# Two attentions on one core: norm scales placed behind the second multiplication, opening output products split, 32-row loads placed ahead of a store

## The chip, the cores and the metric

The kernel runs on one core of a Trainium2 chip. A core has TensorE (PE in the profile), VectorE (DVE), ScalarE (ACT), GpSimd (POOL) and SyncE (SP, which here only issues DMAs). Each has its own queue of instructions, worked through in order, and they meet only through semaphores. The metric is the time of one execution on the device, in microseconds (us); less is better.

## The reference

The input x holds 8 sequences of 512 tokens with 512 channels in fp32. The context holds 8 sequences of 120 tokens, which both attentions read.

```python
x = x + jnp.tanh(g_xattn[0]) * _L0_xattn_ref(_layernorm(x), ctx_1024, ctx_1024, ...)
x = x + jnp.tanh(g_ffn[0])   * _L0_ffn_ref(_layernorm(x), ...)
x = x + jnp.tanh(g_xattn[1]) * _L1_xattn_ref(_layernorm(x), ctx_1024, ctx_1024, mask, ...)
x = x + jnp.tanh(g_ffn[1])   * _L1_ffn_ref(_layernorm(x), ...)

# attention (the second has biases and a key mask besides)
q, k, v = split_heads(Q @ W_q.T), split_heads(K @ W_k.T), split_heads(V @ W_v.T)   # 16 heads of 32
probs = softmax(einsum('bhqd,bhkd->bhqk', q, k) / sqrt(32))
out = einsum('bhqk,bhkd->bhqd', probs, v) @ W_o.T

# first feed-forward: per group of 32 tokens and per expert column, the token with the largest logit
perm = (logits == max(logits over the 32 tokens of the group))
inner = relu(einsum(perm-selected tokens, W1) + b1);  result = perm-scattered (inner @ W2 + b2)

# second feed-forward: a channel mix with a one-token shift
out = sigmoid(xr @ W_r.T) * (square(relu(xk @ W_k.T)) @ W_v.T)
```

## The kernel before

The 4096 tokens are 32 tiles of 128 rows (NT = 32), four to a sequence (TB = 4). x stays on the chip, tokens on the partitions. The two attentions run one after the other and share one class; attention 1 takes about 73 to 430 us of the profiled run and attention 2 about 711 to 1010. Between them lies the routed feed-forward, behind them the channel mix.

**A slot.** Each attention is a loop over tiles; one pass is called a slot, and slot k starts with the scores of tile k on PE. The slots 4 to 27 are `steady(k)`, and the order in which it emits work is the order in each engine's queue: nothing reorders it later. In a slot PE does the scores of tile k (`s`, preceded in attention 2 by a mask product), the output product of tile k-3 (`output`, `ops`: 4 chunks of 128 channels), the query products of a later sequence, transposes of x and of the normalized x (`rxps`, `xnps`), the routing logits (`rlps`), and the product of probabilities and values of tile k-2 (`attend`, `aps`). The number k%4 (f in the code) decides which query products a slot has, so slots differ in length with it.

**The softmax.** The scores lie in two halves, u = 0 and 1. DVE takes the maxima (`largest`, L710), ACT does eight exponentials a half with their sums (L721), DVE takes the reciprocal of the sums (L727), and POOL multiplies the probabilities with it (`divide`, L731). Half 1 goes first: `divide(1)`, then `divide(0)`, the second multiplication of probabilities.

**Turning the probabilities.** For tiles 4 to 25 (`CROSSED`) the probabilities are not transposed on PE. The 120 keys of a head are stored as 4 blocks of 30, each padded to 32. DVE transposes blocks of 32x32 (`turn_blocks`, L793), SP stores the halves to a buffer in device memory (`plane<-pr`, L796), and four loads bring it back with keys on the partitions (`fetch_blocks`, L806, `prT<-plane`), each of 30 rows that lie 4 partitions apart. Half 1 of tile k is turned and stored in slot k, half 0 in slot k+1; then the loads follow. There is one buffer `prT`, so the loads wait until `attend` of the tile before is done; two wide `pr` buffers alternate, so the exponentials of tile k+2 wait until the stores of tile k have landed.

**Queries.** The query products use a scheme with seven products p1 to p7 for a block of 2x2 (Strassen's, in Winograd's form). Its sums fall to POOL (L110, L203, L204) and DVE (L183, L212), and L177 on ACT copies p1. Each product's PSUM tile comes from the same small rotation of banks (`tag="mm"`) as `ops`, `rxps`, `xnps` and `aps`, so each of those waits until the engine that read the bank's last tenant is done.

**Norm scales.** When a tile's output has been added to x, DVE takes its mean and variance (`layernorm_sums`, L52 and L53), and POOL turns them into a scale and an offset with three small instructions (`layernorm_scales`, L61, L62, L64: `ve`, `rstd`, `nmr`). In attention 1 this is `RoutedFfn.in_slot`: at the stage "final" x is put aside to device memory (L1046) and the statistics and scales are made; at the stage "late" ACT applies them in place (`route_scale`, L1052), as the last thing that the slot puts into ACT's queue before the next slot's exponentials. In attention 2 it is `ChannelMix.in_slot`: the statistics come at "final", the scales at "late", four tiles at a time in every fourth slot.

**The opening.** Slot 4 is the first steady one. Before the change it does the whole output of tile 2 in its middle and `attend(3)` at its end; slot 5 does no output in the middle and two chunks of tile 3's output at its end; slot 6 does the other two chunks in its middle; from slot 7 on the pattern is regular.

Of the kernel before, what the change touches and what calls it, by code (L numbers as in the profile page):

```python
# [19 lines left out]
LK = 120  # L20
NH, HD = 16, 32
NT = B * S // P
TB = S // P
NC = D // P
# [8 lines left out]
KB, KF = 4, 30  # L33
# [15 lines left out]
def layernorm_sums(cm, pool, t):  # L49

    st = pool.tile([P, 6], FP, name="bnst")
    cm.nc.vector.bn_stats(st, cm.x[:, t, :])  # L52
    cm.nc.vector.bn_aggr(cm.mv[:, t, :], st)  # L53


def layernorm_scales(cm, pool, t, n):

    nc, ts = cm.nc, slice(t, t + n)
    mean, rstd, nmr = cm.mv[:, ts, 0], cm.rstd[:, ts, 0], cm.nmr[:, ts, 0]
    ve = pool.tile([P, TB], FP, name="ve")[:, :n]  # L60
    nc.gpsimd.tensor_scalar(ve, cm.mv[:, ts, 1], EPS, None, ALU.add)  # L61
    nc.gpsimd.tensor_tensor(rstd, ve, cm.mhalf.to_broadcast([P, n]), ALU.pow)  # L62
    if n == 1:
        nc.gpsimd.tensor_scalar(nmr, mean, rstd, -1.0, ALU.mult, ALU.mult)  # L64
    else:
        nc.gpsimd.tensor_tensor(nmr, mean, rstd, ALU.mult)
        nc.gpsimd.tensor_scalar(nmr, nmr, -1.0, None, ALU.mult)
# [153 lines left out]
class CrossAttention:  # L221
# [566 lines left out]

    def turn_blocks(self, t, u):

        nc = self.nc
        pr = self.probs[t][:, u * 1024 : (u + 1) * 1024]
        nc.vector.transpose(pr, pr)  # L793
        if u == 1:
            self.planes[t] = self.dram.tile([KB, P, 2, 256], FP, name="plane")
        nc.sync.dma_start(  # L796
            out=self.planes[t][:, :, u, :].rearrange("k p e -> p k e"),
            in_=pr.rearrange("p (k e) -> p k e", k=KB),
        )

    def fetch_blocks(self, t):

        prT = self.late.tile([P, 4, 512], FP, name="prT", bufs=1)
        plane = self.planes.pop(t).rearrange("k (q f) u e -> k f q (u e)", q=4)
        for k in range(KB):
            self.nc.sync.dma_start(out=prT[k:LK:KB], in_=plane[k, :KF])  # L806
        self.probs[t] = prT

    def transpose_probs(self, t):
# [118 lines left out]
    def steady(self, k):  # L928

        b, f = divmod(k + TB, TB)  # L930
        crossed = k in CROSSED
        if k == TB:
            self.transpose_probs_late(k - 1)
        largest, exponentials, divide = self.softmax(k, self.score_products(k))
        for u in (1, 0):
            largest(u)
        if k - 1 in CROSSED:
            self.turn_blocks(k - 1, 0)
        done = {TB: TB - 2, TB + 1: None}.get(k, k - 3)
        if done is not None:  # L940
            self.output(done, range(2 if done == TB - 1 else 0, NC))
        exponentials(1)
        divide(1)
        if done is not None:
            self.after(done, "final")
        exponentials(0, range(4))
        if f == 0:
            self.begin_queries(b)
        self.q7.postponed = True
        self.q7.next()  # L950
        exponentials(0, range(4, 8))
        if crossed:
            self.turn_blocks(k, 1)
        self.q7.settle(1)
        divide(0)
        if f != TB - 1:
            self.q7.next()
        if f == 0:
            self.sum_tokens(2)
        self.q7.settle()  # L960
        self.after(k, "route")
        if k + 8 < NT:
            self.transpose_x(k + 8)
        if k == TB:
            self.attend(k - 1)
        elif k == TB + 1:
            self.output(TB - 1, range(2))
        else:
            self.attend(k - 2)
        if k - 1 in CROSSED:  # L970
            self.fetch_blocks(k - 1)
        if k + 9 < NT:
            self.normalize(k + 9)
        if done is not None:
            self.after(done, "late")

    def tail(self):

        for k in range(NT - TB, NT + 2):
            self.transpose_probs_late(k - 2)  # L980
            rest = self.scores(k) if k < NT else []
            self.output(k - 3, range(NC))
            self.after(k - 3, "final")
            self.after(k, "head")
            for part in rest:
                part()
            self.after(k, "route")
            self.attend(k - 2)
            self.after(k - 3, "late")
            self.after(k, "end")  # L990
        self.output(NT - 1, range(NC))
        self.after(NT - 1, "final")
        self.after(NT - 1, "late")
        self.after(NT + 2, "end")


class RoutedFfn:
# [42 lines left out]

    def route_stats(self, t):
        layernorm_sums(self.cm, self.route, t)
        layernorm_scales(self.cm, self.route, t, 1)

    def put_aside(self, t):
# [53 lines left out]
    def in_slot(self, s, attention, stage):  # L1099

        if stage == "final":
            self.put_aside(s)
            self.route_stats(s)
        if stage == "late":
            self.route_scale(s)
        if stage == 2 and 0 <= s - 1:
            self.route_stats(s - 1)
            self.route_norm(s - 1)
        if stage not in (1, "route"):
            return  # L1110
        pool = attention.p_mm
        if s == -1:
            self.start()
        if stage == "route":
            s -= 1
        if 0 <= s - 4:
            self.route_logits(s - 4, pool.tile([P, D], FP, name="rlps", tag="mm"))
        if 0 <= s - 3:
            self.route_x(s - 3, pool.tile([P, D], FP, name="rxps", tag="mm"))
        b, i = divmod(s - 8, TB)  # L1120
        if i == 0 and 0 <= b < B - 2:
            self.route_back(b, pool.tile([P, D], FP, name="pps", tag="mm"))
# [256 lines left out]
class ChannelMix:  # L1379
# [56 lines left out]
    def in_slot(self, s, attention, stage):  # L1436

        nc = self.nc
        self.at = attention
        if stage == 2 and s >= 1:  # L1440
            attention.stats(s - 1)
        if stage == "final" and s < NT - 2 * TB:
            attention.stats(s, False)
        if stage == "late" and s < NT - 2 * TB:
            attention.scales(s)
        if s == -1:
            self.start()
        if stage == "head" and s == NT:
            self.sum_value_weights()
            self.k7.next()  # L1450
        if stage == "end" and s == NT + 1:
            for c in range(NC):
                self.mix_chunk(0, 0, c)
            self.k7.next()
        if stage == "end" and s == NT + 2:
            for step in self.sum_steps(0, 0):
                step()
            self.k7.next(2)
            self.sum_gate_weights()
            for t in range(TB, 2 * TB):  # L1460
                self.normalize(t)
        if stage != "route":
            return
        if s == TB + 1:
            nc.vector.tensor_scalar(self.om, self.mu, -1.0, 1.0, ALU.mult, ALU.add)
        i = s - (NT - 9)
        if 0 <= i - 1 < TB:
            self.transpose(i - 1)
        if 0 <= i < TB:
            xn = self.at.norm.tile([P, D], FP, name="xn")  # L1470
            self.normalize(i, xn)
        if s == NT - 4:
            wv = self.at.pool.tile([P, NC, D], FP, name="wv", tag="wq")
            self.wv = self.load(wv, self.ins[2])
            self.weight_sums = self.sum_key_weights()
        if 0 <= s - (NT - 5) < NC:
            self.mix_chunk(0, 1, s - (NT - 5))
        if s in (NT - 4, NT - 3):
            for _ in range(2):
                self.weight_sums.pop(0)()  # L1480
        if s == NT - 2:
            self.key_sums = self.sum_steps(0, 1, nc.gpsimd)
        if s in (NT - 2, NT - 1):
            for _ in range(2):
                self.key_sums.pop(0)()
        if s == NT - 1:
            self.k7 = self.keys(0)
            self.k7.next()
        if s in (NT, NT + 1):
            self.k7.next()  # L1490
# [336 lines left out]
```

## Time and profile before

| | us |
|---|---|
| median of 3 runs | 1346.75 (1345.57 to 1349.14) |
| the profiled execution | 1344.31 |
| its span | 1342.5 |
| PE busy | 1291.0 (96%) |
| DVE busy | 1002.2 (75%) |
| ACT busy | 807.1 (60%) |
| POOL busy | 704.6 (52%) |
| mean granted TensorE clock | 0.999 |

The profile comes from one execution, whose own time is the 1344.31 us; the span is the stretch between its first and last recorded instruction. An engine's busy time says how long it worked, not whether its work was on the path that sets the end: for that one reads who waited for whom. In lines of the timeline the columns are start (us), duration (us), engine, source line, operation, output<-inputs, shapes and count; in square brackets stands how long the engine had been idle before it, and what released it. Small idle times are partly lost in the modelled ends of PE's instructions.

Lengths of the slots 8 to 24 in this execution, start of scores to start of scores:

| k%4 | attention 1 | attention 2 |
|---|---|---|
| 0 | 10.96 (10.52 in slot 24) | 9.73 (9.88 to 10.48 in slots 12, 16 and 24) |
| 1 | 11.39 | 9.73 |
| 2 | 11.86 (12.5 in slots 10 and 18) | 9.73 |
| 3 | 9.23 | 8.04 to 8.43 |

### The profile page before, as it was taken

The page shows a single profiled execution, that of the slowest core. Times are in us where ns is not written, and L with a number is a line of the kernel's source. Part 1 is how long each engine was busy: PE and PEld are TensorE (multiplying, and loading weights), DVE is VectorE, ACT ScalarE, POOL GpSimd, SP SyncE. Part 2 cuts the span into 40 slices and gives each one's busy share as a digit, 9 for nine tenths or more (in the row PEclk, how much of TensorE's full clock was granted, in tenths as well). Part 3 has the DMA queues.
Part 4 walks back from the last instruction along what each step waited for, and adds up shares of the span by engine and source line. Part 5 has one row for each costly group of instructions (what it writes and reads, how often), then busy time and mean ns, then how long its engine had stood idle before and what let it go on. Part 6 is the DMA issues. An engine that isn't in the chain of part 4 may idle for free. (4 is left out here: it accounts for less than half of the span.)

```text
span 1342.5 us, 32823 instructions
## 1 busy us (share of the span) xinstructions
PE 1291.0 (96%) x13184; PEld 1024.3 (76%) x13184; DVE 1002.2 (75%) x1448; ACT 807.1 (60%) x2540; POOL 704.6 (52%) x626
## 2 busy tenths in 40 slices
PE   7999999999999988999999999999999999999997
PEld 6886777777766877888888667667666888888886
DVE  5876776777685776777887687777785778787776
ACT  1368888888774445455136778888774655544442
POOL 4856655565542002555797787777664333343332
PEclk9999999999999999999999999999999999999999
DMA  9501766766603256431410077767700000000000
GB/s 313 189 1 66 224 208 204 222 211 208 198 26 111 86 171 199 128 112 63 154 47 18 33 229 214 220 212 222 223 23 1 16 17 32 32 32 32 32 32 32
DMA packets 116237, 160.84 MB, mean 120 GB/s; under 512 B 6973, under 2 KB 71997, under 8 KB 116085
## 3 DMA queue, kind: packets, MB, share of 16 engines
q1 hardware_dynamic: 116085, 158.75, 37.1%
q8 instruction: 104, 1.70, 0.5%
q14 instruction: 48, 0.39, 0.1%
HBM read 93.84 MB, written 64.88 MB: 118 GB/s over the span
## 5 line engine op out<-in xcount | busy, mean ns | idle before, releaser
L721 ACT ACTIVATE pr<-s,nmx 128x120 f32<-128x120 f32 x768 | 273.5, 498 | 43.4 <-DVE nmx L710 25.1
L878 PE MATMUL ops<-wo,aT 128*128 128x512 f32 x512 | 237.0, 604 | 3.6 <-ACT aT L869 2.3
L731 POOL TENSOR_TENSOR pr<-pr,rs 128x960 f32<-128x960 f32 x88 | 160.1, 1820 | 139.9 <-DVE rs L727 138.0
L721 ACT ACTIVATION_READ_ACCUMULATOR pr<-s,nmx 128x1 f32 x768 | 195.3, 254 | 0.0
L878 PEld LDWEIGHTS ops<-wo,aT 128*128 128x128 f32 x512 | 91.9, 189 | 99.8 <-issue 89.2
L710 DVE TENSOR_REDUCE nmx<-s 128x8 f32<-128x960 f32 x96 | 106.6, 1153 | 57.9 <-PE s L666 57.8
L1353 POOL TENSOR_TENSOR r<-r,b 128x1024 f32<-128x1024 f32 x31 | 73.5, 2377 | 145.1 <-ACT r L1352 145.1
L793 DVE STREAM_TRANSPOSE pr<-pr 128x1024 f32<-128x1024 f32 x88 | 109.1, 1240 | 37.0 <-POOL pr L731 37.0
L165 PE MATMUL qps<-xnT,wq 128*128 128x256 f32 x512 | 119.0, 380 | 0.0
L165 PEld LDWEIGHTS qps<-xnT,wq 128*128 128x128 f32 x512 | 96.3, 189 | 23.3 <-issue 10.3
L52 DVE BATCH_NORM_STATS2 bnst<-x 128x6 f32<-128x512 f32 x128 | 87.5, 684 | 0.4
L1609 POOL TENSOR_TENSOR x<-x,cv 128x512 f32<-128x512 f32 x30 | 44.0, 1466 | 79.0 <-DVE cv L1606 79.0
L759 POOL TENSOR_TENSOR pr<-pr,rs 128x960 f32<-128x960 f32 x32 | 58.1, 1823 | 40.6 <-DVE rs L758 30.8
L861 PE MATMUL aps<-prT,v 120*32 120x128 f32 x2048 | 69.2, 276 | 7.6 <-DMA prT<-plane 3.9
L888 DVE SCALAR_TENSOR_TENSOR x<-ops,gates,x 128x512 f32<-128x512 f32 x64 | 47.8, 746 | 34.5 <-PE ops L878 34.1
L666 PE MATMUL s<-kT,qT 32*128 32x120 f32 x2048 | 71.8, 276 | 0.0
L666 PEld LDWEIGHTS s<-kT,qT 32*128 32x128 f32 x2048 | 65.7, 186 | 7.0 <-issue 4.9
L861 PEld LDWEIGHTS aps<-prT,v 120*32 120x32 f32 x2048 | 52.2, 109 | 21.2 <-issue 10.7
L1352 ACT COPY r<-rps 128x1024 f32<-128x1024 f32 x31 | 31.4, 1013 | 59.1 <-PE rps L1340 59.1
L1582 ACT ACTIVATE kT<-kT 128x512 f32<-128x512 f32 x32 | 20.0, 626 | 76.2 <-DVE kT L183 41.8
L1340 PE MATMUL rps<-ident,rT 128*128 128x128 f32 x512 | 61.9, 275 | 2.0 <-DVE rT L1320 1.7
L769 ACT ACTIVATE pr<-s,nmx 128x120 f32<-128x120 f32 x128 | 44.2, 371 | 29.0 <-DVE nmx L766 29.0
(239 smaller groups left out, 3134.4 us busy)
## 6 DMA issues: line engine op xcount, KB each, us to landing
plane<-pr SPq DMA_DIRECT2D x88, 512.0 KB, 3.5
prT<-plane SPq DMA_DIRECT2D x176, 240.0 KB, 4.1
w<-in_w_dram SPq DMA_DIRECT2D x32, 512.0 KB, 5.0
x<-in_x_dram SPq DMA_DIRECT2D x8, 1024.0 KB, 16.6
aside<-x SPq DMA_DIRECT2D x32, 256.0 KB, 3.1
x<-aside SPq DMA_DIRECT2D x8, 1024.0 KB, 9.7
out_dram<-x SPq DMA_DIRECT2D x14, 512.0 KB, 2.8
wk<-in_wk_dram SPq DMA_DIRECT2D x3, 1024.0 KB, 8.8
```

The costliest lines, as they stand in the source:

```text
L52: cm.nc.vector.bn_stats(st, cm.x[:, t, :])
L165: self.nc.tensor.matmul(ps[:, m, :], rows[:, k, m * n : (m + 1) * n], columns[:, k, :], start=(k == 0), stop=(k == 1),)
L666: nc.tensor.matmul(s[j // 2][:, j % 2, hc * LK : (hc + 1) * LK], self.qT[b][r : r + 32, hc, toks], self.kT[r : r + 32, hc, keys], start=no ...
L710: nc.vector.tensor_reduce(nmx[u], sv[u], AX.X, ALU.max, negate=True)
L721: nc.scalar.activation(dst, src, AF.Exp, bias=nmx[u][:, j, hc, :], accum_out=sm[:, u, j, hc : hc + 1],)
L731: nc.gpsimd.tensor_tensor(half[u], half[u], by, ALU.mult)
L759: nc.gpsimd.tensor_tensor(pr[:, js, :, :], pr[:, js, :, :], rs[:, js, :, :].to_broadcast([P, 2, NC, LK]), ALU.mult,)
L793: nc.vector.transpose(pr, pr)
L861: nc.tensor.matmul(out, self.v[b // 2][:LK, b % 2, h * HD : (h + 1) * HD], p, start=True, stop=True,)
L878: nc.tensor.matmul(ops, self.aT[t][:, c, :], self.wo[:, c, :], start=(c == 0), stop=(c == NC - 1),)
L1340: nc.tensor.transpose(ps[:, k // 4, (k % 4) * P : (k % 4 + 1) * P], self.rT[:, 16 * tq + 8 * h + k, :], self.cm.ident,)
L1353: nc.gpsimd.tensor_tensor(r, r, b2, ALU.add)
```

## The change

Three things move. The three POOL instructions of the norm scales leave their place right behind the first multiplication (attention 1) or the slot's end (attention 2), and come right behind the second multiplication, at a new stage "scales". At the opening, the output of tile 2 is split: chunks 0 and 1 go to the end of slot 4, behind `attend(3)`, and chunks 2 and 3 to the middle of slot 5; what is done with tile 2 after its output follows into slot 5. And the loads take all 32 rows of each block, the padding rows with them, and are issued ahead of the store of the present tile's half 1, where they had been issued behind it. The line numbers in the changed file are higher by up to 16 (`route_scale` is L1066 there).

```diff
@@ -788,12 +788,17 @@
 
     def turn_blocks(self, t, u):
 
-        nc = self.nc
         pr = self.probs[t][:, u * 1024 : (u + 1) * 1024]
-        nc.vector.transpose(pr, pr)
+        self.nc.vector.transpose(pr, pr)
+        if u == 0:
+            self.store_blocks(t, u)
+
+    def store_blocks(self, t, u):
+
+        pr = self.probs[t][:, u * 1024 : (u + 1) * 1024]
         if u == 1:
             self.planes[t] = self.dram.tile([KB, P, 2, 256], FP, name="plane")
-        nc.sync.dma_start(
+        self.nc.sync.dma_start(
             out=self.planes[t][:, :, u, :].rearrange("k p e -> p k e"),
             in_=pr.rearrange("p (k e) -> p k e", k=KB),
         )
@@ -803,7 +808,7 @@
         prT = self.late.tile([P, 4, 512], FP, name="prT", bufs=1)
         plane = self.planes.pop(t).rearrange("k (q f) u e -> k f q (u e)", q=4)
         for k in range(KB):
-            self.nc.sync.dma_start(out=prT[k:LK:KB], in_=plane[k, :KF])
+            self.nc.sync.dma_start(out=prT[k::KB], in_=plane[k])
         self.probs[t] = prT
 
     def transpose_probs(self, t):
@@ -936,12 +941,12 @@
             largest(u)
         if k - 1 in CROSSED:
             self.turn_blocks(k - 1, 0)
-        done = {TB: TB - 2, TB + 1: None}.get(k, k - 3)
-        if done is not None:
-            self.output(done, range(2 if done == TB - 1 else 0, NC))
+        done = k - 3
+        if k > TB:
+            self.output(done, range(0 if k > TB + 2 else 2, NC))
         exponentials(1)
         divide(1)
-        if done is not None:
+        if k > TB:
             self.after(done, "final")
         exponentials(0, range(4))
         if f == 0:
@@ -953,6 +958,8 @@
             self.turn_blocks(k, 1)
         self.q7.settle(1)
         divide(0)
+        if k > TB:
+            self.after(done, "scales")
         if f != TB - 1:
             self.q7.next()
         if f == 0:
@@ -963,15 +970,17 @@
             self.transpose_x(k + 8)
         if k == TB:
             self.attend(k - 1)
-        elif k == TB + 1:
-            self.output(TB - 1, range(2))
-        else:
+        elif k > TB + 1:
             self.attend(k - 2)
+        if k < TB + 2:
+            self.output(k - 2, range(2))
         if k - 1 in CROSSED:
             self.fetch_blocks(k - 1)
+        if crossed:
+            self.store_blocks(k, 1)
         if k + 9 < NT:
             self.normalize(k + 9)
-        if done is not None:
+        if k > TB:
             self.after(done, "late")
 
     def tail(self):
@@ -981,6 +990,7 @@
             rest = self.scores(k) if k < NT else []
             self.output(k - 3, range(NC))
             self.after(k - 3, "final")
+            self.after(k - 3, "scales")
             self.after(k, "head")
             for part in rest:
                 part()
@@ -990,6 +1000,7 @@
             self.after(k, "end")
         self.output(NT - 1, range(NC))
         self.after(NT - 1, "final")
+        self.after(NT - 1, "scales")
         self.after(NT - 1, "late")
         self.after(NT + 2, "end")
 
@@ -1040,6 +1051,9 @@
 
     def route_stats(self, t):
         layernorm_sums(self.cm, self.route, t)
+        self.route_scales(t)
+
+    def route_scales(self, t):
         layernorm_scales(self.cm, self.route, t, 1)
 
     def put_aside(self, t):
@@ -1100,7 +1114,9 @@
 
         if stage == "final":
             self.put_aside(s)
-            self.route_stats(s)
+            layernorm_sums(self.cm, self.route, s)
+        if stage == "scales":
+            self.route_scales(s)
         if stage == "late":
             self.route_scale(s)
         if stage == 2 and 0 <= s - 1:
@@ -1441,7 +1457,7 @@
             attention.stats(s - 1)
         if stage == "final" and s < NT - 2 * TB:
             attention.stats(s, False)
-        if stage == "late" and s < NT - 2 * TB:
+        if stage == "scales" and s < NT - 2 * TB:
             attention.scales(s)
         if s == -1:
             self.start()
```

## The prediction

> **What bounds the kernel now.** First the page's busy shares: is one engine the wall?
>
> ```profile
> PE 1291.0 (96%) x13184; PEld 1024.3 (76%) x13184; DVE 1002.2 (75%) x1448; ACT 807.1 (60%) x2540; POOL 704.6 (52%) x626
> ```
>
> TensorE (PE) idles about 51 of 1342.5 us, and the change takes no product away: only PE's gaps can shrink or grow. So the second view is the list of waits, PE's rows alone:
>
> ```profile
> PE aps L861 <- DMA prT<-plane: 3.9, 4, 1.7
> PE aps L861 <- DVE qT L212: 3.3, 4, 0.8
> ...
> PE ops L878 <- ACT aT L869: 2.3, 4, 0.7
> ...
> PE s L656 <- ACT pr L721: 1.6, 2, 1.4
> ...
> PE ops L878 <- ACT rxT L1067: 1.2, 1, 1.2
> PE xnps L588 <- ACT xnT L192: 1.0, 1, 1.0
> ```
>
> The columns are total, times, longest. These rows, about 13 us, are all that the change can reach. The timeline places them. The qT waits are in attention 1, in slots 10, 14, 18 and 22, those with k%4 = 2, called f2 here (f0, f1, f3 likewise). The xnT and rxT waits are in slot 5. The DMA waits are in attention 2, in slots 6, 7, 19 and 27. Third, the timelines around slot 10 (start 175.85), GpSimd (POOL), VectorE (DVE) and PE:
>
> ```profile
> 182.28 1.82 POOL L731 TENSOR_TENSOR pr<-pr,rs 128x960 f32<-128x960 f32 x1 [6.96 <-DVE rs L727]
> 184.19 0.22 POOL L61 TENSOR_SCALAR ve<-mv 128x1 f32<-128x1 f32 x1
> 184.50 0.57 POOL L62 TENSOR_TENSOR rstd<-ve,mhalf 128x1 f32<-128x1 f32 x1
> 185.17 0.27 POOL L64 TENSOR_SCALAR nmr<-mv,rstd 128x1 f32<-128x1 f32 x1
> 185.39 1.18 POOL L203 TENSOR_TENSOR qT<-qT,xnT 128x512 f32<-128x512 f32 x1
> 186.54 1.82 POOL L731 TENSOR_TENSOR pr<-pr,rs 128x960 f32<-128x960 f32 x1
> ...
> 186.61 0.69 DVE L212 TENSOR_TENSOR qT<-qT,qps 128x512 f32<-128x512 f32 x1 [1.14 <-POOL qT L203]
> ...
> 187.35 1.08 PE L861 MATMUL aps<-prT,v 120*32 120x128 f32 x32 [0.83 <-DVE qT L212]
> ```
>
> Read upward: aps takes over the PSUM bank that L212 reads, L212 waits for L203, and L203 stands on POOL behind the three scales. They take 1.30 us from the end of the multiplication (184.10) to the end of L64 (185.44). Fourth, attention 2's opening on PE:
>
> ```profile
> 770.40 0.38 PE L656 MATMUL s<-mbias,ones 1*128 1x480 bf16 x2 [1.38 <-ACT pr L721]
> ...
> 779.13 1.08 PE L861 MATMUL aps<-prT,v 120*32 120x128 f32 x32 [1.66 <-DMA prT<-plane]
> ```
>
> Here a load lands too late. Its four issues take 0.84 us each on SP's queue, landing a median 4.1 us behind their issue.
>
> **Scales behind divide(0), attention 1.** Same three instructions, same 1.30 us, other place. What goes: in f2 slots L203 follows the first multiplication directly, ends 1.3 us earlier, and L212 then waits for no POOL. The PE gap there is 0.90 us against PE's own pace (two records share it in the view), four times: -3.6 us. Next late behind it is the reciprocal L727 on DVE, done 1.14 us before L212 started, so the whole gap goes.
>
> What comes: ScalarE's (ACT) route_scale (L1052 before, L1066 after) needs nmr, and stands in ACT's queue right ahead of the next slot's 16 exponentials. Before, it started 1.33 us into the slot, and the first exponential at 2.43 with 0.29 us of slack (slot 12: 198.93 and 200.02). After, nmr is ready 1.30 us behind the end of divide(0). In f0, f1 and f2 divide(0) ends 10.86 into slots of 10.96, 11.39 and (without its gap) 10.96: nmr at 1.20, 0.77 and 1.20 of the next slot, inside 1.33. No loss. But an f3 slot lasts only 9.23: nmr comes 10.87 + 1.30 - 9.23 = 2.93 into the f0 slot. L1066 runs 2.96 to 3.7 there, and the exponentials start 3.66 instead of 2.43: 1.23 late.
>
> What is queued behind: 5.6 us of exponentials and a q copy, then DVE's reciprocal of block 0 (8.80 before, 9.88 after, because an output's stt and the transpose already hold it some way back) and L183, which frees the bank of that slot's aps: L183 ends at 10.6, and aps starts there instead of at 9.95. So +0.67 at slots 12, 16 and 20: +2.0. At slot 8, slot 7's exponentials already start at 3.05, 0.4 later than normal: +1.05. At slot 24 no xn product is left and the banks turn differently: 0. Sum of this edit: -3.6 + 2.0 + 1.05 = -0.55, between -3.6 (the delay hides in the slot) and +2.6 (five handovers of 1.23 paid in full, 6.15, less 3.6).
>
> **Scales in attention 2.** Every fourth slot, one group of about 1.95 us (four columns a time) moves from behind L204 to ahead of it. POOL's total up to the next multiplication is the same, and its reader is several slots off: 0.
>
> **Output products at the opening.** The whole output row (8 products, 3.70 us) leaves slot 4; two chunks (1.72) come to its end, and two to slot 5. Work is unchanged, so only waits count. In attention 1, slot 4's first q product starts at 114.69 instead of 118.22. Then aps needs the bank that ACT's L177 copies out until 121.72, and starts 121.75; the two chunks need the bank that L1067 empties at 123.57, so they end at about 125.3, where slot 5 now starts (123.66 before): +1.65. ACT idles through it. Slot 5's waits on xnT and rxT hang on ACT, which is late itself, so they stay: slot 6 starts 136.0 instead of 134.6, +1.4. DVE's statistics and L1066 of tile 2 move a slot on with it, beside this wait. Bounds: 0 (ACT catches up) and +1.65.
>
> In attention 2 the mask product of slot 6 starts 0.48 earlier (no ACT wait of 1.4 against more output work ahead of it), but its exponentials are held by DVE's maxima at the same time as before: 0 by itself.
>
> **Loads of 32 rows, ahead of the store.** Four loads per tile as before, 256 KB for 240. SP's order becomes aside, four loads, store of block 1. In slot 6 of attention 2 the store (waiting for DVE's transpose) held the loads until 771.46; now they go at about 769, when the previous aps has released prT. With an unchanged 4.1 us from issue to landing, the last lands at 773 to 776, before PE wants it at 776.87. Slot 6 then ends when its exponentials do, 0.41 us earlier; slot 7's load wait (1.20) goes too, slot 8 being bound by exponentials: -1.2 kept at slot 9. Slot 27: -0.8, PE follows directly. Slots 11 to 23: the load's gap of up to 0.43 only uncovers the exponentials, which end 8.3 into f3 slots of 8.04 to 8.43 and hold the next mask product; together -0.1. Sum -2.1, between -0.5 (only slot 27 gains, and not wholly) and -4.4 (all load gaps).
>
> How long does a 32-row issue last? No 32-row load of this shape is in the trace: loads of 120 rows issue in 0.47 to 0.58, of 128 rows in 0.33 to 0.44, the 30-row ones in 0.84. I take 0.37, being divisible like 128; the dear end (0.84) costs 0.4 of the 2.1. The store of block 1 now waits behind loads that wait for prT; the exponentials two tiles later need it landed (3.5 us), and by replay have over 3 us to spare even at the dear end.
>
> [...] If landing did shrink with the issue, attention 2 would still be held by its exponentials.
>
> **Sum.** The profiled run took 1344.31 us (span 1342.5), 2.4 below the median of 1346.75. Attention 1: -0.55 + 1.4 = +0.85. Attention 2: -2.1. Together about -1.3: 1343.0 for that run, 1345.5 for a median. A measurement of this kernel can tell about 0.3% (4.0 us) from no change.
>
> **Rivals.**
> *Gaps go, nothing comes.* The bank of aps in f0 slots is free in time, and the opening catches up: -3.6 - 2.1 = -5.7, 1341.0. For it: ACT is busy only 60%, and the exponentials end 1.3 us before their slot does. Against: L183's place behind the reciprocal.
> *The hand-over on ACT becomes the bound (slower).* Place: route_scale ahead of the first exponential. It decides in every slot once nmr is later than 1.33 + 0.29 = 1.62 into it; f0 and f2 come to 1.20, so 0.42 us of drift is enough, and f1 inherits part of f0's delay. Price: five full handovers, 6.15, the opening 1.65, less 3.6 and 2.1: +2.1 (1348.9); with 0.3 us in each of the other 15 slots 4.5 more: +6.6 (1353.4). Middle: 1351. Against: ACT's slack in the rows above.
> *The loads do not do what they say.* Issue stays dear and they wait for prT as long as for the store; slot 6 and 7 keep their gaps, only slot 27 gains: +0.85 - 0.8, 1346.8, no change.
>
> **How the numbers follow.** Forecast 0.50, gaps go 0.24, ACT bound 0.18, loads idle 0.08. Faster by over 0.3% (below 1342.7): most of the second case (0.21) and the forecast's lower edge (0.04), 0.25. Slower (above 1350.8): half of the third and a little of the forecast, 0.13. The rest, 0.62, within. The unknowns' cheap ends add up to -3.6 - 4.4 = -8.0 (1338.8), the dear ends to +2.6 + 1.65 - 0.5 = +3.8 (1350.5); with the third case's middle, 8 in 10 lie in 1339.0 to 1351.0.
>
> **What would show it.** Right: no wait of aps on L212; ops or aps of slots 8, 12, 16, 20 waiting 0.6 to 1.1 on L183; first exponentials of those slots at about 3.7 with L1066 waiting for L64; slot 5 starting about 1.6 later; no load waits; 32-row issues near 0.37. Wrong: f0 slots of 10.96 as before, first exponentials later than 2.5 in f1 to f3 slots, PE waiting for loads, or exponentials waiting for the store's landing.

## The result and the profile after

The changed kernel takes 1357.44 us (1356.41 to 1358.59, 4 runs) against 1347.45 us for the kernel before in the same comparison: ratio 1.0076, interval 1.0063 to 1.0088. It is about 10 us slower. The profiled execution took 1356.41 us with a span of 1354.6, 12.1 above the span of before.

The busy time of PE, the first line of the page again, against 1291.0 before:

```profile
PE 1296.5 (96%) x13184; PEld 1027.4 (76%) x13184; DVE 1001.9 (74%) x1448; ACT 807.4 (60%) x2540; POOL 705.0 (52%) x626
```

The matmuls are the same 13184, but busy for 5.5 us longer: PE's clock fell somewhere (in slot 4 of attention 1 and slot 12 of attention 2, see below). The list of waits of the changed kernel, PE's rows that answer to those shown of before (us in total, times, longest):

```profile
PE aps L866 <- DMA prT<-plane: 7.8, 7, 1.8
...
PE aps L866 <- DVE qT L183: 3.2, 4, 1.2
...
PE aps L866 <- ACT qT L177: 2.5, 1, 2.5
...
PE ops L883 <- ACT aT L874: 1.9, 3, 0.7
...
PE ops L883 <- ACT rxT L1081: 1.3, 2, 0.7
```

The row on L212 is gone and one on L183 has come, both as forecast. The wait for loads should have gone and has doubled. And SP's own list has a row at 156.2 us that was 3.0 us before. First the two rows of before, then those of the changed kernel:

```profile
SPq L806 <- PE aps L861: 32.2, 24, 2.5
...
SPq L806 <- DMA plane<-pr: 3.0, 2, 2.7
```

```profile
SPq L811 <- DMA plane<-pr: 156.2, 66, 6.3
...
SPq L811 <- PE aps L866: 22.8, 15, 2.1
```

Loads now wait for a store to land. Before, they waited for `aps` to release `prT` (24 times) and for the store only twice.

From the start of each slot in the two traces, where the 12.1 us lie:

| stretch | before | after | difference | forecast |
|---|---|---|---|---|
| slots 4 and 5, attention 1 | 21.02 | 25.62 | +4.6 | +1.4 |
| slots 6 to 27, attention 1 | 236.79 | 237.17 | +0.4 | -0.55 |
| slots 4 to 8, attention 2 | 47.17 | 45.84 | -1.3 | -1.2 |
| slots 9 to 26, attention 2 | 170.46 | 178.95 | +8.5 | -0.1 |

Slot 27 of attention 2 adds 0.4, where -0.8 was forecast; what is left (-0.4) lies outside the changed slots. Two stretches make the loss: the steady slots of attention 2, and the opening of attention 1.

### The profile page after: what moved, and what is told of

Read it like the earlier page. It is cut to its first block, busy times and chain, and to the rows that moved or that the text cites. A ratio compares the mean times of both kernels' runs of the same rounds, so it can differ in the third digit from the quotient of the medians.

```text
span 1354.6 us, 32824 instructions
## 1 busy us (share of the span) xinstructions
PE 1296.5 (96%) x13184; PEld 1027.4 (76%) x13184; DVE 1001.9 (74%) x1448; ACT 807.4 (60%) x2540; POOL 705.0 (52%) x626
## 5 line engine op out<-in xcount | busy, mean ns | idle before, releaser
L721 ACT ACTIVATE pr<-s,nmx 128x120 f32<-128x120 f32 x768 | 273.8, 499 | 42.6 <-DVE nmx L710 29.3
L883 PE MATMUL ops<-wo,aT 128*128 128x512 f32 x512 | 240.4, 610 | 4.5 <-ACT aT L874 1.9
L1366 DVE TENSOR_TENSOR r<-rps,b 128x1024 f32<-128x1024 f32 x33 | 40.4, 1225 | 28.3 <-PE rps L1356 28.3
```

Source lines behind the costliest of these rows:

```text
L721: nc.scalar.activation(dst, src, AF.Exp, bias=nmx[u][:, j, hc, :], accum_out=sm[:, u, j, hc : hc + 1],)
L883: nc.tensor.matmul(ops, self.aT[t][:, c, :], self.wo[:, c, :], start=(c == 0), stop=(c == NC - 1),)
```

## The experiments

**The ring on SP's queue.** First SP's timeline in the steady slots of attention 2, of the changed kernel (start us, duration us, then the issues merged):

```profile
883.75 2.53 SPq L811 DMA_DIRECT2D prT<-plane  x4
886.33 1.14 SPq L801 DMA_DIRECT2D plane<-pr  x2
893.72 2.54 SPq L811 DMA_DIRECT2D prT<-plane  x4
896.29 1.14 SPq L801 DMA_DIRECT2D plane<-pr  x2
903.66 1.88 SPq L811 DMA_DIRECT2D prT<-plane  x3
```

and of the kernel before:

```profile
846.59 3.71 SPq L806 DMA_DIRECT2D prT<-plane  x4
851.12 4.62 SPq L796 DMA_DIRECT2D plane<-pr  x2
856.23 3.48 SPq L806 DMA_DIRECT2D prT<-plane  x4
```

Before, the two stores are issued 4 us apart, each as soon as DVE has turned its half (the merged 4.62 spans that). After, both stand behind the loads and go out together, and then SP has nothing to do for 6.3 us. The landing times in the trace close the circle: the second of these stores (half 0) is issued at 886.96 and lands at 893.60, and the next loads go at 893.72. In each of the 21 turns of attention 2 the loads start 0.07 to 0.21 us behind that landing. Before, a store landed a median 3.5 us behind its issue, now 5.8. Loads were still under way at the issue of 42 of the 88 stores before (those landed in a median 3.9 us, the others in 3.0) and at that of 82 now (5.8, the others 2.9). So there is a ring: loads, store of half 1, store of half 0, its landing, next loads. It turns once in 9.93 us on average over slots 9 to 25, where the slots 9 to 26 of attention 2 averaged 9.47 before. In attention 1 a slot lasts 10.9 on average and the ring has time to spare.

Four kernels take the change apart, one step each. The first puts the store back:

```diff
             self.turn_blocks(k, 1)
+            self.store_blocks(k, 1)
...
-        if crossed:
-            self.store_blocks(k, 1)
```

> The changed kernel with the store of half 1 issued ahead of the loads again; scales, opening and 32 rows as changed. Theory (a ring on SP's queue in attention 2: four loads, store of half 1, store of half 0, its landing, next loads, 9.9 us a tile against slots of 9.3 on average): the ring is cut, slots f0 to f2 of attention 2 return to 9.73 and f3 to 8.0 to 8.4, about 9 us less, 1348 to 1349. Rival (the 32-row loads themselves, with more bytes, land later): stays at 1355 or more. Store landing falls from 5.8 to about 3.5 us by the theory.

Measured: 1350.47 us, ratio 1.0011 (0.9999 to 1.0023). Slots 9 to 26 of attention 2 take 170.35 us, the store lands in 3.4, and SP waits 2.0 us in all for a store. Its list, in the row that had 156.2:

```profile
SPq L811 <- DMA plane<-pr: 2.0, 1, 2.0
```

The ring is cut by the order alone. The second is the kernel before with the new order and nothing else, 30 rows a load:

```diff
         if k - 1 in CROSSED:
             self.fetch_blocks(k - 1)
+        if crossed:
+            self.store_blocks(k, 1)
```

> The kernel before with nothing but the loads (of 30 rows) issued ahead of the store of half 1. Theory (ring): with issues of 0.84 us instead of 0.60 the ring gets longer, 4 x 0.9 + 0.8 + 6.2 = 10.6 us a tile, against 9.3 in attention 2: about +20 us, 1365 to 1372; attention 1 (10.9 a slot) hardly moves. Rival (32-row loads): no loss, 1346 to 1348.

Measured: 1353.99 us, ratio 1.0036 (1.0022 to 1.0051): slower, but by 5.5 us and not 20. The ring is there (SP's row stands at 140.1 us), but turns in 9.67, faster than with 32 rows: 173.43 us for slots 9 to 26. The theory had the sign right and the size wrong: it added the issue times, but the ring with the issues of 0.84 us is the shorter one. With 30 rows the last load lands 6.86 us behind the first issue, though the issues take 3.47 us; with 32 rows 7.10 us, though they take 2.53. The shorter issues brought the four loads in no sooner.

Whether bytes make the ring was asked by adding a store of 256 KB behind the store of half 1, in the changed kernel and, as a control, in `order_back`:

```diff
             self.store_blocks(k, 1)
+            self.store_extra(k)     # half of the turned half 1, to a spare buffer
```

> The changed kernel with one store more per crossed tile: 256 KB of the turned half 1 go to a spare buffer right behind its store, so between the loads and the store of half 0. Theory (the ring is a batch of bytes: 2 MB of loads and stores between two landings in 9.85 us, about 258 GB/s behind 1.9 us of latency): the ring grows by 256 KB / 258 = 1.0 us to about 10.9, attention 2's 19 crossed slots cost +18 us, about 1375; attention 1 (10.9 a slot) loses a few us at most. Rival (the wait is a fixed latency of the landing): no more than the issue, 0.4 us a slot, +7.

> The same extra store in the kernel with the store of half 1 ahead of the loads (order_back). Theory: there the store lies outside the stretch between loads and the store of half 0, its bytes overlap the wait for DVE and PE, and the slots stay at 9.73 and 8.0: 1350 to 1354. Rival (the DMA engines are simply full): attention 2 grows by 10 us or more here too.

Measured: in the changed kernel 1372.71 us from two executions, ratio 1.0175 (1.0141 to 1.0209) against 1.0076; the ring turns in 10.50 on average, 0.57 more, and slots 9 to 26 take 189.64 us. In the control they take 171.66, 1.3 above `order_back`, though the same bytes flow. Its whole time is 1355.38 us, ratio 1.0042 (1.0013 to 1.0072) against 1.0011. In its profile 2.9 us of that lie in slots 4 to 8 of attention 2 (51.03 against 48.12): PE waits 3.22 us there behind DVE's reciprocal, and the granted clock is then 0.50 for 6.83 us, against 3.41 in `order_back`. The 256 KB cost 0.57 and not the 1.0 expected, so the 258 GB/s, an estimate from 2 MB in 9.85 us less 1.9 (a load of 16 KB, `b<-in_b_dram`, landed in 1.9 in the kernel before), is too slow a rate for what is added; that place in the ring is what makes bytes dear is shown, an exact price isn't.

Last, 32 rows with the bytes of 30, in the kernel with the new order:

```diff
-            self.nc.sync.dma_start(out=prT[k:LK:KB], in_=plane[k, :KF])
+            self.nc.sync.dma_start(out=prT[k::KB, :, :480], in_=plane[k, :, :, :480])
```

> The kernel before with the loads ahead of the store, 32 rows but 480 of their 512 columns, so 240 KB each as with 30 rows; one head's probabilities of 16 are left out (another head's are read in their place). With 30 rows the period of the ring in attention 2 was 9.67 us a tile on average, with 32 rows 9.93. Theory (bytes): 9.6 to 9.7. Rival (rows, engines or the faster issue): 9.9 or more.

Measured: the ring turns in 9.70 on average (9.67 with 30 rows, 9.93 with all of 32). The whole kernel took 1351.81, ratio 1.0013 (1.0001 to 1.0024). So it is the 64 KB more of padding per tile that made the ring 0.26 longer, neither the rows nor the pace of the issues. Neither of the other two edits accounts for the 0.26: the kernels `split_back` and `scales_back` below, with 32 rows and one of these edits taken back each, have rings of 9.98 and 9.97. Why the whole kernel comes out below `order_only` (1.0036) stays open; its slots 9 to 26 take 174.56 us, 1.1 more. The 32 rows alone, in the kernel before:

```diff
-            self.nc.sync.dma_start(out=prT[k:LK:KB], in_=plane[k, :KF])
+            self.nc.sync.dma_start(out=prT[k::KB], in_=plane[k])
```

> The kernel before with nothing but the 32-row loads, still behind the store of half 1. Theory: there is no ring, the issue falls from 0.84 to 0.60 us, four loads land at most 0.5 us earlier, attention 2 changes by -0.5 to 0: 0.999 to 1.000. Rival (32 rows themselves are slow, as their pairs of landings in the changed kernel suggest): +1 us or more in attention 2, waits of aps on the loads.

Measured: 1348.94 us, ratio 1.0002 (0.999 to 1.0013); slots 9 to 26 of attention 2 take 170.28. Outside a ring they are worth nothing in time, although the last of the four loads lands 6.53 us behind the first issue there (median in attention 2), against 7.07 before.

**The opening.** In the changed kernel slot 4 of attention 1 takes 13.75 us, where the forecast had 11.7. Its windows (length; busy of PE, PEld, DVE, ACT, POOL with instructions; granted clock; DMA share, GB/s):

```profile
123.00:124.00 1.00, 0.46 (x5) 0.27 (x2) 1.00 (x3) 1.00 (x5) 0.36 (x1) 0.50 0.00 0
124.00:125.00 1.00, 1.00 (x2) 0.48 (x3) 0.11 (x1) 1.00 (x3) 1.00 (x1) 0.50 0.55 196
125.00:126.00 1.00, 1.00 (x2) 0.42 (x2) 0.00 (x0) 0.36 (x1) 1.00 (x2) 0.50 0.95 328
126.00:127.00 1.00, 1.00 (x2) 0.00 (x0) 0.00 (x0) 0.00 (x0) 0.92 (x2) 0.50 0.01 1
127.00:128.00 1.00, 1.00 (x9) 0.56 (x12) 0.00 (x0) 0.00 (x0) 0.83 (x2) 0.50 0.00 0
```

The granted clock is 0.50 from 122.58 to 129.41, for 6.83 us. The four output products take 3.78 us where they take 1.98 at full clock (below), and ACT and DVE stand still for them:

```profile
121.87 1.31 PE L866 MATMUL aps<-prT,v 120*32 120x128 f32 x32 [2.49 <-ACT qT L177]
123.73 3.78 PE L883 MATMUL ops<-wo,aT 128*128 128x512 f32 x4 [0.54 <-ACT rxT L1081]
```

PE's wait of 2.49 us for L177 comes just before the fall, the one of 0.54 for L1081 lies within it. Was it the waits? One kernel takes the split back:

```diff
-        done = k - 3
-        if k > TB:
-            self.output(done, range(0 if k > TB + 2 else 2, NC))
+        done = {TB: TB - 2, TB + 1: None}.get(k, k - 3)
+        if done is not None:
+            self.output(done, range(2 if done == TB - 1 else 0, NC))
...
-        if k < TB + 2:
-            self.output(k - 2, range(2))
+        elif k == TB + 1:
+            self.output(TB - 1, range(2))
```

> The changed kernel with the opening of before. Theory (PE idles 2.5 us in slot 4 and then runs at half clock for some 6 us): slot 5 of attention 1 starts 3.7 and slot 6 4.6 us earlier, granted clock 1.00 there; 1357.4 - 4.6 + what the opening in attention 2 gave = about 1353. Rival (only the 1.4 us of the prediction): 1356.

Measured: 1359.01 us, ratio 1.0070 (1.005 to 1.009), no gain that the times could tell from the changed kernel. Slots 4 and 5 of attention 1 take 22.38, 3.24 less than 25.62, but slot 5 takes 12.31 where it took 10.95 before. The granted clock is 1.00 there; PE waits for POOL instead:

```profile
128.24 1.99 PE L165 MATMUL qps<-xnT,wqs 128*128 128x256 f32 x8 [1.06 <-POOL xnT L110]
```

This kernel still has the scales behind `divide(0)`, and at the end of slot 4 they now stand ahead of L110 in POOL's queue, which starts 3.00 us into slot 5 instead of 1.67. In the changed kernel slot 4 has no scales. So this test moved two things, and the 1.36 us more in its slot 5 come from the scales standing there. In slot 6 of attention 2 the granted clock did fall to 0.50, for 3.41 us, where it had not fallen in the changed kernel.

In the opening of before the clock can fall as well: slot 5 took 11.93 to 12.65 in the profiles of `order_only`, `order32_less`, `rows32_only` and of both runs of the best kernel below, each with a granted clock of 0.50 for 3.41 us, though their slots 4 and 5 are those of before, which had shown 10.95. So one profile of before flattered it. The other test leaves the split and gives PE something to do in its wait:

```diff
             nc.tensor.transpose(ps[:, c, :], xn[:, c * P : (c + 1) * P], self.cm.ident)
+        if t == TB + 8 and not self.masked:
+            for c in list(range(NC)) * 5:
+                nc.tensor.transpose(ps[:, c, :], xn[:, c * P : (c + 1) * P], self.cm.ident)
```

> The changed kernel with 20 transposes more in slot 4 of attention 1: the four transposes of xn are done five times over into the same bank with the same result, in PE's 2.5 us wait for L177. Theory (PE idle for 2.5 us makes the granted clock fall to 0.50 for about 6 us): PE stays busy, the clock stays 1.00, aps starts at the same time, and slot 4 takes 11.7 to 12.0 instead of 13.0 to 13.75, slot 6 starts about 2.5 to 3 us earlier. Rival (the output products are slow for another reason, such as the bank): nothing changes, or slower by the added 2.2 us.

Measured: 1354.00 us, ratio 1.0030 (1.0015 to 1.0044) against 1.0076 for the changed kernel, with 20 instructions more. PE's timeline of `warm`:

```profile
119.23 2.35 PE L591 MATMUL xnps<-ident,xn 128*128 128x128 f32 x20
121.86 1.08 PE L869 MATMUL aps<-prT,v 120*32 120x128 f32 x32 [0.29 <-ACT qT L177]
123.72 1.98 PE L886 MATMUL ops<-wo,aT 128*128 128x512 f32 x4 [0.78 <-ACT rxT L1084]
```

`aps` starts when it did, at 121.86; the four products now take 1.98, not the 3.78 of the changed kernel; slot 4 lasts 11.93 and slots 4 and 5 take 22.87. Its profiled execution ran 1356.78, above its median, with a dip of the clock in attention 2 (mean granted clock 0.996). A clean case came by accident: `extra_back` has the same slot 4 without the extra transposes, the same waits (2.47 and 0.78), and in its profile the clock stayed up:

```profile
122.59 1.08 PE L875 MATMUL aps<-prT,v 120*32 120x128 f32 x32 [2.47 <-ACT qT L177]
124.44 1.98 PE L892 MATMUL ops<-wo,aT 128*128 128x512 f32 x4 [0.78 <-ACT rxT L1090]
```

So the split costs 1.85 us in itself (22.87 against 21.02), close to the forecast; the fall of the clock adds 2.75 more in the profile shown, and it does not come in each execution. Where it came on both sides, slots 4 and 5 took 23.96 to 25.62 us with the split and 22.00 to 22.72 with the opening of before.

Why the same wait slows the clock in one profile and not in another can be read from the traces. In each of the 14 profiles, wherever the granted clock changes more than once, the changes lie whole multiples of 3.413 us apart (122.58, 129.41, 832.55 and 835.97 us in the changed kernel), and a fall lasts one such step or two (the one at the program's end aside). Two steps of this grid around the wait, in the changed kernel and in `extra_back`:

```profile
119.17:122.58 3.41, 0.92 (x30) 0.71 (x32) 0.55 (x2) 3.41 (x20) 1.82 (x1) 1.00 0.01 2
122.58:126.00 3.42, 2.88 (x19) 1.33 (x8) 1.53 (x3) 2.79 (x8) 2.36 (x2) 0.50 0.44 153
```

```profile
118.23:121.65 3.42, 1.89 (x13) 1.49 (x11) 0.20 (x1) 3.42 (x23) 0.56 (x1) 1.00 0.00 0
121.65:125.06 3.41, 1.70 (x34) 1.19 (x35) 1.88 (x3) 3.41 (x16) 1.97 (x2) 1.00 0.01 2
```

In the changed kernel the whole wait, 2.49 us, lies in one step, and the next step runs at 0.50. In `extra_back` the wait falls on two steps with 1.53 and 1.71 us of idle time, and the clock stays. Between 20 and 1330 us of the 14 profiles, 9 of 9 steps at full clock with more than 2.0 us of idle PE were followed by one at 0.50 (in the changed kernel the one from 119.17 us, with 2.49), 17 of 90 with 1.2 to 2.0 us (there the one from 829.14 us, with 1.83), and none with less. In these profiles a fall thus goes with the idle time within one step, for which the place of a wait on the grid counts beside its length; what decides between 1.2 and 2.0 us stays open.

**The scales.** The fourth kernel puts the three POOL instructions back where they were, in both attentions.

```diff
         if stage == "final":
             self.put_aside(s)
-            layernorm_sums(self.cm, self.route, s)
-        if stage == "scales":
-            self.route_scales(s)
+            self.route_stats(s)
...
-        if stage == "scales" and s < NT - 2 * TB:
+        if stage == "late" and s < NT - 2 * TB:
             attention.scales(s)
```

> The changed kernel with the scales at their old places. Theory: slots 8, 12, 16, 20 of attention 1 lose their wait on L183 (1.3 + 3 x 0.72), slots 10, 14, 18, 22 get 0.90 back each, about equal: 1357 within 1. Rival (the late scales hold up more than those slots): 1354 or less.

Measured: 1358.86 us, ratio 1.0066 (1.0052 to 1.008) against 1.0076, as expected no difference. Its slots 6 to 27 of attention 1 take 236.77 us, against 237.17. The two effects are both there in the changed kernel; its ACT and PE in slot 12, which starts at 202.65:

```profile
205.63 0.81 ACT L1066 ACTIVATE x<-x,nmr,rstd 128x512 f32<-128x512 f32 x1 [1.55 <-POOL nmr L64]
206.35 0.45 ACT L721 ACTIVATE pr<-s,nmx 128x120 f32<-128x120 f32 x1
```

```profile
213.31 1.08 PE L866 MATMUL aps<-prT,v 120*32 120x128 f32 x32 [0.65 <-DVE qT L183]
214.32 1.17 PE L666 MATMUL s<-kT,qT 32*128 32x120 f32 x32
```

L1066 starts 2.98 us into the slot and the first exponential at 3.70 (forecast 2.96 and 3.66); `aps` waits for L183, and the slot lasts 11.68 instead of 10.96 (+0.72, forecast +0.67).

**A version meant to keep the gains.** The kernel before, with the scales behind `divide(0)` in attention 1 only where they pay (f2 slots; in attention 2 they stay at the changed kernel's place), and the loads ahead of the store only in slots 5 and 6 of attention 2; opening and rows as before:

```diff
             self.after(done, "final")
+            if f != 2 and not self.masked:
+                self.after(done, "scales")
...
         divide(0)
+        if done is not None and (f == 2 or self.masked):
+            self.after(done, "scales")
...
+        ahead = self.masked and k in (TB + 1, TB + 2)
+        if crossed and not ahead:
+            self.store_blocks(k, 1)       # the place of before
...
+        if crossed and ahead:
+            self.store_blocks(k, 1)       # behind fetch_blocks
```

> The kernel before with two things: the scales of attention 1 behind divide(0) in f2 slots alone, and the loads ahead of the store in slots 5 and 6 of attention 2 alone (30 rows). Theory: -0.90 in slots 10, 14, 18, 22, and 1.2 us in attention 2's opening, no wait on L183, no ring: -4.8, ratio about 0.9965. Rival (dips of the granted clock swallow it): 0.998 to 1.000.

Measured: 1343.52 us, ratio 0.9961 (0.9946 to 0.9977). Slots 6 to 27 of attention 1 take 233.13 us, 3.66 less than before, and slots 9 to 26 of attention 2 take 170.34: no ring. The gain in attention 2's opening was mostly not kept: slots 4 to 8 take 46.79 us (47.02 when run again) against 47.17, where 1.2 less was expected. Slot 6 takes 9.74 instead of 11.49, but slot 8 takes 10.96 instead of 9.73, with a wait of `aps` for its loads (0.93). Run again, the same kernel beside a version that keeps PE busy in slot 5:

```diff
-        for c in range(NC):
+        for c in list(range(NC)) * (3 if t == 1 else 1):
             cols = slice(c * P, (c + 1) * P)
             nc.tensor.transpose(ps[:, cols], self.cm.x[:, t, cols], self.cm.ident)
...
             nc.tensor.transpose(ps[:, c, :], xn[:, c * P : (c + 1) * P], self.cm.ident)
+        if t == TB + 9 and not self.masked:
+            for c in list(range(NC)) * 2:
+                nc.tensor.transpose(ps[:, c, :], xn[:, c * P : (c + 1) * P], self.cm.ident)
```

> The best kernel so far once more, for the comparison on one chip: ratio 0.996 to 0.997.

> The best kernel with PE kept busy in its two waits of slot 5 of attention 1: the transposes of x are done three times, those of xn three times, with the same results in the same banks (16 transposes more). Theory (two waits of 1.2 us within 3 us let the granted clock fall in some executions): slot 5 takes 10.9 instead of 12.6 where the clock fell, about 1 us less in the median, 0.995 to 0.996. Rival (no dip there in most executions): same as the other, or slower by up to 0.5.

Measured: 1344.94 us, ratio 0.9966 (0.9954 to 0.9978), and 1343.59 us, ratio 0.9955 (0.9939 to 0.9971). In the two profiles slot 5 takes 12.56 without and 10.95 with the added transposes. The direction is that of the theory, but the two intervals overlap: the gain of the second in time is not shown.

## Why the prediction was wrong

- **Scales, what goes.** Right: slots 10, 14, 18 and 22 are shorter by 0.90 to 0.91, in sum 3.6; the best kernel has just this gain. (The working's 1.30 us from 184.10 to 185.44 is 1.34; nothing hangs on it.)
- **Scales, what comes.** Right in mechanism, a little small in size. Slots 12, 16 and 20 became longer by 0.72 to 0.73 each, slot 8 by 1.31 where 1.05 was forecast, and slot 25 by 0.55 that the working did not have: at slot 24 nothing waits, but its exponentials start 3.71 in, the scales behind its `divide(0)` come late into slot 25, and there `aps` waits 0.48 for L188. The delay was inherited by one slot more than was followed.
- **Opening, attention 1.** The waits were right: `aps` at 8.18 us into slot 4 (forecast 8.16), the output products at 10.04 (9.98). The term that was mis-sized is what PE does after them: two chunks were priced at 1.72 us, from rows at full clock, and took 3.78. The step did not ask whether 2.49 us of waiting leave the clock as it is. Part of the +4.6 is luck of the profile before, whose opening ran at full clock where five others with the same opening did not.
- **Attention 2's opening.** Right: -1.3 for -1.2, and for the reason given, the store no longer standing ahead of the loads. The split had no part in it: `order_only`, without the split, takes the same 45.84 us.
- **Loads ahead of the store.** This step failed, and it decides the sign. The working named what is queued behind the waiting loads, the store of half 1, and asked only one of those who wait for it, the exponentials two tiles later; those indeed show no wait for a store. It did not ask what stands behind that store: the store of half 0 of the same tile, for whose landing the next loads wait. It also kept the store's landing at 3.5 us, a median over 88 stores, of which 46 were issued with no load under way. In the trace of before the sum could have been made: four issues 3.5, two issues of stores 0.7 and a landing of 3.5 come to 7.7, inside a slot but close enough to ask what the landing would become. In the ring the store of half 0 goes out 3.2 us behind the first load and lands 6.6 us later: 9.8, above the 9.47 of the slots. The forecast -0.1 for slots 9 to 26 became +8.5.
- **The 32-row issue.** It takes 0.60 us, between the 0.37 taken and the 0.84 bound, and was worth nothing. The 0.37 was an estimate from the loads of 128 rows; no run shows that divisibility sets the time of an issue. That landing stays at a median 4.1 us was the author's estimate too. Outside a ring it came no sooner: in `rows32_only` the fourth load lands 4.57 us behind its own issue, against 4.26 before, and only the shorter issues bring the four in sooner (6.53 against 7.07 behind the first issue, medians in attention 2). In the ring 64 KB more took 0.26 us more.
- **The rivals.** The slower one put its price on ACT's hand-over; its rows show no such thing beyond slots 8 to 25 as listed. That the loads would do nothing was too kind to them. No rival had a queue that waits for itself: the range ended at 1351.0, and all of slower had 0.13.

## What to carry to other kernels

When a step moves in an in-order queue that also waits, follow the queue round: what is behind it, what is behind that, and whether the last of them is what the first waits for next time. If so, the stages have a period of their own, and it has to be set against the shortest average of the loop it serves; a latency measured with less under way ahead is no price for it (here 3.5 us became 5.8). And where an edit leaves TensorE a wait like the 2.49 us here, price the work behind it at half clock as well: the granted clock fell to 0.50 in four of the five profiles with this wait, and in the fifth the wait lay on two steps of the clock's grid.

## What the runs showed of the hardware

- A store of 512 KB landed a median 3.5 us behind its issue in the kernel before, where two stores were issued a median 4.3 us apart (3.0 with no load under way, 46 of 88 stores), and 5.8 (6.0 in attention 2) in the changed kernel, where loads were under way at the issue of 82.
- The granted clock changed on a grid of 3.413 us in all profiles, and fell to 0.50 for one or two steps of it. It fell after a wait of 2.49 us within one step, and did not after a wait of 2.47 us spread over two, in another kernel with the same instructions there. In the changed kernel it fell in slot 12 of attention 2 as well (832.55 to 835.97 us), behind a wait of 1.83 us for loads; that is part of the 8.5.
- Loads of 32 rows were issued in 0.60 us, those of 30 rows in 0.84. Four of them landed 0.54 us sooner outside the ring, and no sooner in it (7.10 against 6.86 us behind the first issue).
